# Recurrence in one round per seed pair: seeds for two rounds in one bank, additions split 22 to 10, eight output buffers, and a seam check of two instructions a half

## The chip, the cores and the metric

The kernel runs on one core of one Trainium2 chip. The metric is the time of one execution on the device, in microseconds (us). The engines have short names in the profile: PE is the matrix engine (PEld its weight loads), DVE the vector engine, ACT the scalar engine, POOL the GpSimd engine, SP the engine that issues most of the transfers (DMA). PSUM is the memory that matmuls write to[...]. SBUF is the working memory.

## What is computed

Two layers over `x` of 4 x 128 x 64 x 64. Layer 0 is a windowed attention with a depthwise convolution ahead of it. Layer 1 is a linear attention and then a recurrence over the 4096 tokens of each image, and only this last part is concerned here:

```python
def _L1_ffn_ref(x, W, V, gamma, beta):
    ...
    Wx = jnp.einsum('bti,hi->bth', x, W)
    flat = Wx.reshape(B * T, H)
    mean = jnp.mean(flat, axis=0)
    var = jnp.var(flat, axis=0)
    Wx = ((flat - mean) * jax.lax.rsqrt(var + BN_EPS) * gamma + beta).reshape(B, T, H)
    Vt = V.T
    def step(yt, wx_t):
        yt = jax.nn.sigmoid(wx_t + yt @ Vt)
        return (yt, yt)
    y0 = jnp.zeros((B, H), dtype=Wx.dtype)
    _, ys = jax.lax.scan(step, y0, jnp.swapaxes(Wx, 0, 1))
    return jnp.swapaxes(ys, 0, 1)
...
t = t + _L1_ffn_ref(_ln_t(t), L1_ffn_W, L1_ffn_V, L1_ffn_gamma, L1_ffn_beta)
```

The mean and variance run over all tokens, so the recurrence can't start before the rest of the kernel has ended.

## The kernel before

The first 856 us, up to L733 (`main.close()`), hold layer 0 and the linear attention, in 64 windows whose instructions stand in an order that the kernel fixes for each engine (`in_order`, L732). That part leaves two things behind. `wx` in SBUF holds the products of the recurrence's input, laid out as [channel, image, piece, step, run of 16]. `resd` in device memory holds the values to which the recurrence's outputs are added.

What the diff touches is the rest, from L740 on, whose instructions the build may place by itself within each engine's queue.

**Loads and statistics.** `res` (8 MB) is read back from `resd` by four transfers of one image each (L748), two on SP's queue, two on ACT's. DVE and POOL turn the gathered statistics into a factor `sc` and an offset `shift` for each channel (L754 to L761).

**Cutting the recurrence.** The 4096 steps of an image are cut into 128 segments of 32 steps (`SEGS`, `SEG`). All segments of all four images advance together: one round is one step of 4 x 128 = 512 columns, each with 128 channels on the partitions. Segment k would need the end of segment k-1 as its start, which isn't there yet; so it starts 11 steps (`WARM`) ahead, at step 21 of the segment before, from nothing, and runs 11 warm rounds that produce no output. The state has then forgotten its start. Of the warm result, shifted by one segment (the tiles `warm` have one column more, column 0 being zero for the true start), 32 counted rounds follow. At the end the state reached by each segment is compared with the warm start of the next (the seam): where any differs by more than `TOL`, a flag sends the program to a slower general version (L849), which doesn't run in these executions.

**A round.** The 512 columns are two groups of 256 (`NG`, images 0 and 1, images 2 and 3). For each, DVE writes `wx * sc + shift` of that step into a bank of PSUM (the seed, `seeded`, L771), PE adds the product of the previous state with `fvT` onto it (L803 warm, L815 counted), and ACT writes the sigmoid (L806 and L817), which is the next state. While ACT works on one group, PE can work on the other. A group has three banks, of which a seed uses half. [...]

**Output of a counted round.** POOL adds `res` and `ys` for images 0 to 2 (384 columns), DVE for image 3 (128), into `ot` (L822), and SP sends `ot` to device memory (L823, 256 KB). `ys` and `ot` come from the pool `ring` with three buffers each. An addition waits until the transfer of three rounds before has read its `ot`; a sigmoid waits until the additions of three rounds before have read its `ys`; and DVE takes its instructions in order, so seeds placed behind a waiting addition wait too.

**The end.** For each group DVE runs four instructions of 256 columns: difference, square, comparison, sum (L830 to L833). One small matmul (L840) sums over the partitions, L842 and L844 make the flag `bad`, all engines load it (L847), and the program ends.

## Time and profile before

| what | value |
|---|---|
| median of 6 runs | 931.58 us (927.58 to 934.5) |
| the profiled execution | 930.36 us |
| its span, first to last instruction | 928.5 us |
| PE, DVE, ACT, POOL busy over the span | 94%, 80%, 58%, 28% |
| last transfer of `res` landed | 879.04 us |
| seeds L771 | 86, mean 541 ns (128 x 256) |
| counted sigmoids L817 | 64, mean 385 ns (128 x 256) |
| additions L822, POOL / DVE | 32 each, mean 1080 ns (128 x 384) / 324 ns (128 x 128) |
| seam check L830, L831, L832, L833 | 2 each, mean 522, 750, 286, 413 ns |

The stage of the change by stretches, in us from the span's start. Columns: PE, PEld, DVE, ACT and POOL busy, each with its number of instructions, the TensorE clock that was granted, the DMA engines' busy share, GB/s moved:

```profile
856.50:860.30 3.80, 1.31 (x6) 0.59 (x4) 2.63 (x7) 1.49 (x2) 0.75 (x2) 0.50 0.92 315
860.30:879.90 19.60, 17.34 (x54) 9.25 (x54) 14.89 (x30) 10.80 (x28) 2.89 (x3) 0.87 0.86 368
879.90:888.50 8.60, 7.20 (x26) 3.99 (x26) 8.60 (x22) 4.51 (x12) 5.08 (x5) 1.00 0.49 191
888.50:899.60 11.10, 10.10 (x37) 5.83 (x36) 10.23 (x28) 6.81 (x18) 10.24 (x11) 1.00 0.60 233
899.60:917.50 17.90, 14.61 (x54) 7.82 (x52) 15.32 (x39) 9.97 (x26) 14.30 (x14) 1.00 0.49 192
917.50:922.50 5.00, 0.54 (x4) 0.09 (x2) 4.12 (x11) 0.76 (x2) 1.78 (x2) 0.76 0.40 157
```

The rows are: statistics; warm rounds and the first counted ones, while `res` loads; the rounds just behind that load; the middle; the rest of the rounds; the end. A timeline row gives the start, the time from its first to its last instruction, the engine, the line, what it writes and reads, and in brackets how long the engine was idle before it and what ended that. A row of the chain of waits gives start, length, and the engine and line that the end of the kernel went through.

### The profile page before, as it was taken

To read this page: it belongs to the slowest core of one execution; us is meant where nothing else is said; L and a number is where in the kernel's file an instruction comes from. 1 tells how busy PE (TensorE), PEld (TensorE's weight loads), DVE (VectorE), ACT (ScalarE), POOL (GpSimd) and SP (SyncE) were. 2 spreads that over 40 slices of the span, in tenths; PEclk is the share of its full clock that TensorE was granted. 3 is DMA by queue.
4 is the path that set the end of the run, shared out by engine and by line. 5 is a ranking of instruction groups with operands and counts; after the bars stand their busy time and mean duration, and the time that the engine had idled before them with its cause. 6 is when DMAs were issued, how large, how long until landed. Compare 5 with 4: busy or idle time off the path is not lost.

```text
span 928.5 us, 26534 instructions
## 1 busy us (share of the span) xinstructions
PE 872.0 (94%) x10508; PEld 652.3 (70%) x10508; DVE 740.3 (80%) x2452; ACT 540.1 (58%) x1010; POOL 260.2 (28%) x359
## 2 busy tenths in 40 slices
PE   4978999999999999999999999999999999977884
PEld 3856777777777877777787877787777777755442
DVE  6455979888797978797988889797879786677796
ACT  3655666565756566666656575656666665523553
POOL 2122131423232232313132323223231412121185
PEclk9989999999999999999999999999999999999898
DMA  4112121122212111212112121212121111101853
GB/s 121 28 44 62 37 78 42 48 57 63 60 62 59 50 54 49 73 38 81 41 49 58 59 59 60 60 51 58 48 71 40 58 37 60 32 35 51 349 217 136
DMA packets 53045, 63.46 MB, mean 68 GB/s; under 512 B 22960, under 2 KB 33840, under 8 KB 52400
## 3 DMA queue, kind: packets, MB, share of 16 engines
q1 hardware_dynamic: 51184, 56.91, 19.6%
q10 hardware_dynamic: 1728, 4.77, 1.3%
q8 instruction: 85, 1.39, 0.6%
q14 instruction: 48, 0.39, 0.1%
HBM read 35.44 MB, written 17.30 MB: 57 GB/s over the span
## 4 chain that ended last, share of the span: by engine, by line
PE 60%; DVE 24%; DMA 5%; ACT 4%; issue 3%; POOL 3%; ACTq 0%; DVEq 0%; SPq 0%; POOLq 0%
PE bank L337 8%; DVE y L288 8%; PE bank L382 6%; PE bank L465 6%; PE bank L212 6%; PE bank L494 4%; PE bank L400 4%; PE bank L350 4%; PE bank L412 4%; PE bank L602 3%; DMA res<-resd 2%; PE bank L573 2%; PE bank L537 2%; DVE st L191 2%; PE bank L575 2%
## 5 line engine op out<-in xcount | busy, mean ns | idle before, releaser
L288 DVE SCALAR_TENSOR_TENSOR y<-ypad,cpe_w,y 128x512 f32<-128x512 f32 x240 | 190.5, 794 | 16.8 <-ACT y L286 13.4
L391 ACT ACTIVATE es<-bank 128x512 f32<-128x512 f32 x256 | 132.4, 604 | 76.9 <-PE bank L382 76.9
L440 POOL TENSOR_TENSOR oT<-o_sb,rden 128x512 f32<-128x512 f32 x64 | 84.2, 1316 | 243.2 <-DMA rden<-rd 209.7
L195 POOL TENSOR_SCALAR rs<-mv 128x4 f32<-128x4 f32 (+2 forms) x100 | 25.2, 252 | 364.4 <-DVE mv L193 162.5
L203 DVE TENSOR_SCALAR xn<-x,mv,rs 128x128 f32<-128x128 f32 x256 | 88.8, 409 | 26.6 <-POOL rs L196 26.6
L196 POOL TENSOR_TENSOR rs<-rs,mhalf 128x4 f32<-128x4 f32 (+2 forms) x100 | 106.2, 1062 | 8.3
L382 PEld LDWEIGHTS bank<-q,k 32*128 32x128 f32 x3072 | 97.7, 189 | 9.0 <-ACT k L345 7.8
L382 PE MATMUL bank<-q,k 32*128 32x96 f32 (+1 forms) x3072 | 96.3, 270 | 1.1 <-ACT k L345 1.1
L412 PEld LDWEIGHTS bank<-es,v_sb 128*32 128x32 f32 x3072 | 56.5, 110 | 30.1 <-issue 20.3
L465 PE MATMUL bank<-woT,oT 128*128 128x128 f32 x512 | 65.6, 283 | 6.1 <-POOL oT L440 6.1
L494 PE MATMUL bank<-xl,awT 128*128 128x512 f32 x128 | 70.0, 630 | 0.0
L412 PE MATMUL bank<-es,v_sb 128*32 128x96 f32 (+1 forms) x3072 | 69.7, 239 | 0.0
L465 PEld LDWEIGHTS bank<-woT,oT 128*128 128x128 f32 x512 | 62.4, 196 | 10.2 <-POOL oT L440 7.8
L400 PE MATMUL bank<-es,ones 128*32 128x512 f32 x512 | 69.1, 612 | 0.0
L357 ACT COPY v_sb<-bank 128x512 f32<-128x512 f32 x64 | 37.6, 588 | 53.5 <-PE bank L350 45.7
L337 PE MATMUL bank<-y2w,wqT 128*128 128x256 f32 x256 | 67.3, 386 | 1.0 <-DVE y2w L288 1.0
L337 PE MATMUL bank<-y2w,wkT 128*128 128x256 f32 x256 | 66.7, 384 | 0.0
L350 PE MATMUL bank<-wvT,y2w 128*128 128x256 f32 x256 | 66.0, 380 | 0.0
L345 ACT COPY q<-bank 128x512 f32<-128x512 f32 x64 | 37.7, 589 | 40.8 <-PE bank L337 38.9
L345 ACT COPY k<-bank 128x512 f32<-128x512 f32 x64 | 37.4, 585 | 37.5 <-PE bank L337 37.4
L191 DVE BATCH_NORM_STATS2 st<-x 128x6 f32<-128x128 f32 x256 | 55.5, 280 | 1.1
L337 PEld LDWEIGHTS bank<-y2w,wqT 128*128 128x128 f32 x256 | 46.1, 195 | 13.0 <-issue 7.2
(124 smaller groups left out, 1725.1 us busy)
## 6 DMA issues: line engine op xcount, KB each, us to landing
rden<-rd SPq DMA_DIRECT2D x64, 256.0 KB
v_sb<-v_sb SPq DMA_DIRECT2D x128, 64.0 KB
resd<-rs_o SPq DMA_DIRECT2D x32, 256.0 KB
out<-ot SPq DMA_DIRECT2D x32, 256.0 KB
xin<-in_xt SPq DMA_DIRECT2D x15, 512.0 KB
res<-resd SPq DMA_DIRECT2D x2, 2048.0 KB
res<-resd ACTq DMA_DIRECT2D x2, 2048.0 KB
dc<-den SPq DMA_DIRECT2D x64, 8.0 KB
```

The source lines that it names most:

```text
L196: nc.gpsimd.tensor_tensor(rs[:, :n], rs[:, :n], mhalf[:, :n], ALU.pow)
L203: nc.vector.tensor_scalar(xn[:, j, :], piece, mv[:, j, 0:1], rs[:, j : j + 1], ALU.subtract, ALU.mult)
L288: nc.vector.scalar_tensor_tensor(y2, src, cpe_w[:, tap : tap + 1], y2, ALU.mult, ALU.add)
L337: nc.tensor.matmul(pps[:, br * WT : (br + 1) * WT], wT[:, br * P : (br + 1) * P], y2, start=True, stop=True,)
L350: nc.tensor.matmul(vps[:, e * 256 : (e + 1) * 256], y2[:, e * P : (e + 1) * P], wvT, start=True, stop=True,)
L382: nc.tensor.matmul(sps[h][:, cols], w["k"][rows, k0 : k0 + P], w["q"][rows, cols], start=False, stop=(br, n) == pieces[-1],)
L391: nc.scalar.activation(es, sps[h], AF.Exp, scale=scale)
L400: nc.tensor.matmul(dps[rows], ones[:, :HD], w["es", h], start=True, stop=True)
L412: nc.tensor.matmul(ops[rows, cols], w["v"][:, n, c0 : c0 + HD], w["es", h][:, cols], start=(br, n) == pieces[0], stop=(br, n) == pieces[-1],)
L440: nc.gpsimd.tensor_tensor(oTs[n][:, :, :, wj * WS : (wj + 1) * WS], w["o"].rearrange("p (a r c) -> p a r c", a=BR, c=WS), w["rden"].rearra ...
L465: nc.tensor.matmul(yps[:, j * P : (j + 1) * P], oT[:, br, t], woT[:, br, :], start=br == 0, stop=br == BR - 1,)
L494: nc.tensor.matmul(zps, awT[:, m * P : (m + 1) * P], h.xl, start=True, stop=True)
```

## The change

- The first warm round is a sigmoid of ACT straight from `wx`, with `sc` and `shift` as its factor and offset; it has no seed.
- The other 10 warm and the 32 counted rounds stand in one list, `rounds`. For two rounds that follow each other, a group has one seed: one DVE instruction of 512 columns fills both halves of a bank, and the two rounds use a half each. A group still has three banks, seeded in the order of the pairs, up to two pairs ahead in the program's text. The other pool of PSUM has one bank for two.
- Warm rounds write into `ys` of the ring too; only the last of them writes `warm`, which is one tile now, and the `spare` tiles are gone.
- The additions are split by rows of 16 columns: POOL takes 22 of 32 rows (352 columns), DVE 10 (160).
- `ot` has eight buffers. `ys` still has three.
- The seam is compared by two instructions a group, each `(end + TOL >= warm)` or `(end - TOL <= warm)` with the sum of the ones as a second output (`accum_out`). The count that is expected becomes twice as large.

```diff
--- before.py
+++ after.py
@@ -740,8 +740,9 @@
     sp = fast.enter_context(tc.tile_pool(name="sp", bufs=1))
     rec = ExitStack()
     ring = rec.enter_context(tc.tile_pool(name="ring", bufs=3))
-    ps_r = rec.enter_context(tc.tile_pool(name="ps_r", bufs=3, space=PSUM))
-    ps_m = rec.enter_context(tc.tile_pool(name="ps_m2", bufs=2, space=PSUM))
+    ZBUFS = 3
+    ps_r = rec.enter_context(tc.tile_pool(name="ps_r", bufs=ZBUFS, space=PSUM))
+    ps_m = rec.enter_context(tc.tile_pool(name="ps_m2", bufs=1, space=PSUM))
 
     res = sp.tile([P, B, NH, SEG, HSEGS], F32, name="res")
     for b in range(B):
@@ -760,77 +761,108 @@
     nc.vector.tensor_tensor(shift, mv[:, 0:1], sc, ALU.mult)
     nc.vector.tensor_tensor(shift, beta, shift, ALU.subtract)
 
-    NG = 2
-    GB = B // NG
-    GC = GB * SEGS
-
-    def seeded(g, s):
-
-
-        bk = ps_r.tile([P, 512], F32, tag=f"bank{g}", name=f"bank{g}")
-        nc.vector.tensor_scalar(
-            bk[:, :GC].rearrange("p (b n k) -> p b n k", n=NH, k=HSEGS),
-            wx[:, g * GB : (g + 1) * GB, :, s, :],
-            sc,
-            shift,
-            ALU.mult,
-            ALU.add,
-        )
-        return bk[:, :GC]
+
+    rounds = [(s, False) for s in range(SEG - WARM + 1, SEG)] + [(s, True) for s in range(SEG)]
+    COLS = B * SEGS
+    GC = COLS // 2
+    seeds = {}
+
+    def seed(k, g):
+
+
+        if 2 * k < len(rounds):
+            s = rounds[2 * k][0]
+            seeds[k, g] = ps_r.tile([P, 2, GC], F32, tag=f"z{g}", name=f"z{g}")
+            nc.vector.tensor_scalar(
+                seeds[k, g].rearrange("p r (m k) -> p r m k", k=HSEGS),
+                wx[:, 2 * g : 2 * g + 2, :, s : s + 2, :].rearrange("p b n s k -> p s (b n) k"),
+                sc,
+                shift,
+                ALU.mult,
+                ALU.add,
+            )
 
 
     idle = sp.tile([P, 1], F32, name="idle")
     nc.scalar.activation(idle, ones[:, :1], AF.Sigmoid)
 
 
-    for g in range(NG):
-        for _ in range(3):
-            bk = ps_r.tile([P, 512], F32, tag=f"bank{g}", name=f"bank{g}")
+    for _ in range(ZBUFS):
+        for g in range(2):
+            bk = ps_r.tile([P, COLS], F32, tag=f"z{g}", name=f"z{g}")
             nc.tensor.matmul(
-                bk[:, :GC], zeros, zeros[:, :1].to_broadcast([P, GC]), start=True, stop=True
-            )
-
-
-    warm = [sp.tile([P, GB, SEGS + 1], F32, name=f"warm{g}") for g in range(NG)]
-    spare = [sp.tile([P, GB, SEGS + 1], F32, name=f"spare{g}") for g in range(NG)]
-    for g in range(NG):
-        nc.gpsimd.memset(warm[g][:, :, 0:1], 0.0)
-    for s in range(SEG - WARM, SEG):
-        for g in range(NG):
-            z = seeded(g, s)
-            now, was = (warm[g], spare[g]) if (SEG - 1 - s) % 2 == 0 else (spare[g], warm[g])
-            if s > SEG - WARM:
-                nc.tensor.matmul(
-                    z, fvT, was[:, :, 1:], start=False, stop=True, skip_group_check=True
+                bk, zeros, zeros[:, :1].to_broadcast([P, COLS]), start=True, stop=True
+            )
+
+
+    warm = sp.tile([P, B, SEGS + 1], F32, name="warm")
+    nc.gpsimd.memset(warm[:, :, 0:1], 0.0)
+    halves = [(0, GC), (GC, COLS)]
+
+    last = ring.tile([P, COLS], F32, tag="ys", name="ys")
+    for c0, c1 in halves:
+        nc.scalar.activation(
+            last[:, c0:c1].rearrange("p (m k) -> p m k", k=HSEGS),
+            wx[:, c0 // SEGS : c1 // SEGS, :, SEG - WARM, :].rearrange("p b n k -> p (b n) k"),
+            AF.Sigmoid,
+            bias=shift,
+            scale=sc,
+        )
+    for k in range(ZBUFS - 1):
+        for g in range(2):
+            seed(k, g)
+    for r, (s, counts) in enumerate(rounds):
+        seed(r // 2 + ZBUFS - 1, r % 2)
+
+        moved, were_moved = rounds[r] == (SEG - 1, False), rounds[r] == (0, True)
+        ys = None if moved else ring.tile([P, COLS], F32, tag="ys", name="ys")
+        for g, (c0, c1) in enumerate(halves):
+            b = slice(c0 // SEGS, c1 // SEGS)
+            z = seeds[r // 2, g][:, r % 2, :]
+            nc.tensor.matmul(
+                z,
+                fvT,
+                warm[:, b, :SEGS] if were_moved else last[:, c0:c1],
+                start=False,
+                stop=True,
+                skip_group_check=True,
+            )
+            if moved:
+                nc.scalar.activation(
+                    warm[:, b, 1:], z.rearrange("p (b k) -> p b k", k=SEGS), AF.Sigmoid
                 )
-            nc.scalar.activation(
-                now[:, :, 1:], z.rearrange("p (b k) -> p b k", k=SEGS), AF.Sigmoid
-            )
-
-    last = [w[:, :, :SEGS] for w in warm]
-    for s in range(SEG):
-        ys = ring.tile([P, B * SEGS], F32, tag="ys", name="ys")
-        for g in range(NG):
-            z = seeded(g, s)
-            nc.tensor.matmul(z, fvT, last[g], start=False, stop=True, skip_group_check=True)
-            y = ys[:, g * GC : (g + 1) * GC]
-            nc.scalar.activation(y, z, AF.Sigmoid)
-            last[g] = y
-        ot = ring.tile([P, B, NH, HSEGS], F32, tag="ot", name="ot")
-        yv = ys.rearrange("p (b n k) -> p b n k", n=NH, k=HSEGS)
-        for eng, b0, b1 in ((nc.gpsimd, 0, 3), (nc.vector, 3, 4)):
-            eng.tensor_tensor(ot[:, b0:b1], res[:, b0:b1, :, s, :], yv[:, b0:b1], ALU.add)
-        nc.sync.dma_start(out[s].rearrange("p b k -> p (b k)"), ot.rearrange("p b n k -> p (b n k)"))
-
-
+            else:
+                nc.scalar.activation(ys[:, c0:c1], z, AF.Sigmoid)
+        if not moved:
+            last = ys
+        if counts:
+            ot = ring.tile([P, COLS], F32, tag="ot", name="ot", bufs=8)
+            for eng, m0, m1 in ((nc.gpsimd, 0, 22), (nc.vector, 22, 32)):
+                eng.tensor_tensor(
+                    ot.rearrange("p (m k) -> p m k", k=HSEGS)[:, m0:m1],
+                    res[:, :, :, s, :].rearrange("p b n k -> p (b n) k")[:, m0:m1],
+                    ys.rearrange("p (m k) -> p m k", k=HSEGS)[:, m0:m1],
+                    ALU.add,
+                )
+            nc.sync.dma_start(out[s].rearrange("p b k -> p (b k)"), ot)
+
+
+
+    NG = 4
     okc = sp.tile([P, NG + 1], F32, name="okc")
-    for g in range(NG):
-        d = sp.tile([P, GB, SEGS], F32, tag="d", name="d", bufs=2)
-        end = last[g].rearrange("p (b k) -> p b k", k=SEGS)
-        nc.vector.tensor_tensor(d, end, warm[g][:, :, 1:], ALU.subtract)
-        nc.vector.tensor_tensor(d, d, d, ALU.mult)
-        nc.vector.tensor_scalar(d, d, TOL * TOL, None, ALU.is_le)
-        nc.vector.tensor_reduce(okc[:, g : g + 1], d, AX.XY, ALU.add)
+    d = sp.tile([P, COLS], F32, name="d")
+    for i, (b0, b1) in enumerate(((0, 2), (2, B))):
+        end = last[:, b0 * SEGS : b1 * SEGS].rearrange("p (b k) -> p b k", k=SEGS)
+        for k, (side, op) in enumerate(((ALU.add, ALU.is_ge), (ALU.subtract, ALU.is_le))):
+            nc.vector.scalar_tensor_tensor(
+                d[:, b0 * SEGS : b1 * SEGS].rearrange("p (b k) -> p b k", k=SEGS),
+                end,
+                TOL,
+                warm[:, b0:b1, 1:],
+                side,
+                op,
+                accum_out=okc[:, 2 * i + k : 2 * i + k + 1],
+            )
 
     nc.vector.tensor_scalar(dmax, dmax, HUGE, None, ALU.is_le)
     nc.vector.tensor_scalar(dmin, dmin, TINY, None, ALU.is_ge)
@@ -841,7 +873,7 @@
     oks = sp.tile([1, 1], F32, name="oks")
     nc.vector.tensor_reduce(oks, okp[:1, : NG + 1], AX.X, ALU.add)
     bad = sp.tile([1, 1], mybir.dt.int32, name="bad")
-    nc.vector.tensor_scalar(bad, oks, float(P * B * SEGS + P * 16), None, ALU.is_lt)
+    nc.vector.tensor_scalar(bad, oks, float(2 * P * B * SEGS + P * 16), None, ALU.is_lt)
     rec.close()
 
     flag = nc.values_load(bad[0:1, 0:1], min_val=0, max_val=1)
```

## The prediction

> **What bounds the kernel now.** I read the page's engine table and slices first: PE is 94% busy over the whole span, but the slices after about 856 us fall to 7 and 8, so the last 72 us, which is all that the change touches, have another limit. Then the chain of waits for that stretch:
>
> ```profile
> 856.43 22.61 DMA res<-resd
> ...
> 879.13 0.74 DVE ot L822
> ...
> 900.55 1.11 POOL ot L822
> ...
> 901.68 3.83 DMA out<-ot
> ...
> 905.64 0.29 DVE ot L822
> 905.93 0.47 DVE bank L771
> ```
>
> The reader is to see two gates. Up to 879.04 us the load of `res` is last, whatever the rounds do. Later the chain goes twice through an output transfer (3.83 us here, 2.63 us at 909.33), then through DVE's addition and a seed queued behind it. Next, ACT's timeline, which counts rounds (a round is two sigmoids):
>
> ```profile
> 874.05 0.89 ACT L806 ACTIVATE warm<-bank 128x256 f32<-128x256 f32 x2 [0.29 <-PE bank L803]
> 875.25 0.89 ACT L817 ACTIVATE ys<-bank 128x256 f32<-128x256 f32 x2 [0.30 <-PE bank L815]
> 876.42 0.89 ACT L817 ACTIVATE ys<-bank 128x256 f32<-128x256 f32 x2 [0.29 <-PE bank L815]
> 877.59 0.89 ACT L817 ACTIVATE ys<-bank 128x256 f32<-128x256 f32 x2 [0.29 <-PE bank L815]
> 879.99 0.39 ACT L817 ACTIVATE ys<-bank 128x256 f32<-128x256 f32 x1 [1.51 <-DVE ot L822]
> ...
> 898.37 0.76 ACT L817 ACTIVATE ys<-bank 128x256 f32<-128x256 f32 x2 [0.47 <-PE bank L815]
> 899.65 0.77 ACT L817 ACTIVATE ys<-bank 128x256 f32<-128x256 f32 x2 [0.52 <-PE bank L815]
> ...
> 904.70 0.77 ACT L817 ACTIVATE ys<-bank 128x256 f32<-128x256 f32 x2 [0.52 <-PE bank L815]
> 907.30 0.78 ACT L817 ACTIVATE ys<-bank 128x256 f32<-128x256 f32 x2 [1.83 <-PE bank L815]
> ...
> 917.51 0.76 ACT L817 ACTIVATE ys<-bank 128x256 f32<-128x256 f32 x2 [0.46 <-PE bank L815]
> ```
>
> Warm rounds come every 1.17 us. Three counted rounds (s = 0, 1, 2) are done when ACT stops, for `ys` has three buffers and the first is held by an addition that waits for `res`. From s = 3 at 879.99 to s = 31 at 917.51 there are 28 periods in 37.52 us, 1.340 each. Undisturbed ones, 889.74 to 898.37, are 1.233; later short (1.23) and long (1.29) ones alternate, the idle time before them 0.46 and 0.52. One takes 2.60 (904.70 to 907.30). The first six after 879.99 hold 8.51 us, 1.10 more than six of 1.233: DVE then has seeds and additions to catch up on.
>
> Last, DVE's timeline at the end:
>
> ```profile
> 917.93 0.63 DVE L830 TENSOR_TENSOR d<-ys,warm 128x256 f32<-128x256 f32 x1 [0.50 <-ACT ys L817]
> 918.59 1.09 DVE L831 TENSOR_TENSOR d<-d 128x256 f32<-128x256 f32 x1
> 919.60 0.28 DVE L822 TENSOR_TENSOR ot<-res,ys 128x128 f32<-128x128 f32 x1
> ...
> 921.44 0.42 DVE L833 TENSOR_REDUCE okc<-d 128x1 f32<-128x256 f32 x1
> ...
> 922.33 0.14 DVE L844 TENSOR_SCALAR bad<-oks 1x1 int32<-1x1 f32 x1
> ```
>
> Call T the end of the last sigmoid, 917.51 + 0.76 = 918.27. The flag is written at 922.47, T + 4.2; then come 6.0 us of flag load, branch and closing that the change leaves alone (span 928.5).
>
> [...] L831 took 1.09 us beside POOL's last addition (918.40 to 919.40) and 0.41 without it, while seeds beside POOL keep 0.53 to 0.55. [...] In the 3.83 us wait, fifteen of the sixteen had landed by 903.68 and the last at 905.52: a straggler, which a deeper ring absorbs, not a lack of bandwidth. [...] Here L288, that operation without an accumulator, takes 794 ns for 512 columns; no run yet shows it with one.
>
> **Part by part.** *The start.* The first round loses its seeds: ACT takes the sigmoid from `wx` directly once `shift` is there (859.62) instead of at 860.36. Two seeds of 512 columns follow, then round two. A 512-column seed isn't in the trace. The 256-column one takes 541 ns, 470 start to start (4.70 us for ten). DVE's additions grow from 292 ns at 128 columns to 413 at 256, 0.945 ns a column, so 541 + 242 = 783 ns, some 710 start to start. Bounds: 610 (half of the growth) and 940 start to start (twice the old). The first matmul can start at about 860.5, its sigmoid at 861.25, and ten warm periods later, at 873.0, the first counted one: 2.2 us before 875.25. All of it is lost against the load of `res`, which still lands at 879.04: ACT's stop grows from 1.5 to about 3.7 us. I cost the start at nothing. The zeroing matmuls write 512 columns for 256, at most doubling 1.44 us on PE, to 857.8 plus 1.4: they end before the first seed. One POOL memset less is idle time.
>
> *Restart at `res`.* DVE's waiting addition has 160 columns for 128: 292 + 32 x 0.945 = 322 ns, here 0.74 + 0.03 beside POOL. ACT restarts at 880.0 as before, at s = 3.
>
> *DVE in a round.* Before: two seeds and an addition, 2 x 0.45 + 0.20 = 1.10 us start to start, of a period of 1.233: hardly room to catch up. After: one seed and a longer addition, 0.71 + 0.23 = 0.94. Seeds may run up to six rounds ahead instead of three. Of 86 seeds 42 remain. So the catching up of 1.10 us should go: PE finds its seeds ready for the first rounds behind the stop, and DVE has 0.29 us of slack a round. If that slack weren't there, the 1.10 would come back.
>
> *POOL.* 352 columns for 384: between 990 (in proportion) and 1080 ns. It has three rounds before its `ys` is written again, so this saves nothing on the path.
>
> *Eight output buffers.* An addition waits for the transfer of eight rounds before, not three: five more periods, 6.2 us, against a straggler of 1.9. The 2.60 becomes 1.23 (1.37 less), and the 1.40 at 912.35 also (0.17).
>
> *What is late next.* The loop PE, ACT, PE of group 0: sigmoid 0.39, 0.05, load and matmuls 0.70, 0.04, plus 0.06 for a second wait that ACT's first sigmoid of a counted round takes as an instruction of its own, after PE's last matmul. That second wait (for the additions that read `ys`) stays, so 1.233 and not 1.17. The long 1.29 comes where PE's extra wait instruction stands ahead of the weight load. Only every other round of a group waits for a new seed now, so I take the middle of 1.233 and the alternating mean 1.26: 1.247. 28 x (1.340 - 1.247) = 2.6 us less up to T.
>
> *The end.* Eight comparing instructions become four with an accumulator. One of 256 columns is 794 - 256 x 0.945 = 552 ns, about 0.5 start to start[...]. In the order seen before (one on group 0, the second held by POOL's last addition until T + 1.42, DVE's addition, then group 1) : T + 1.5, + 0.25, + 2 x 0.56, + 0.6 for the count on PE and its two small instructions (921.86 to 922.47) is T + 3.4, so 0.8 less. Bounds: [...] T + 2.6 where POOL doesn't hold DVE: 0.1 to 1.6 less. The last transfer would land near T + 3.8, which the closing 6 us cover.
>
> Sum: 2.6 + 0.8 = 3.4 us. The profiled execution took 930.36 (span 928.5 and 1.9 around it): 927.0. The median shown is 931.58, 1.2 above that execution, so 928.2.
>
> **Rivals.**
> - *The loop gets faster* (1.17 a round): half of PE's seed waits go, and the order of ACT's waits may change. For: warm rounds run so, with the same matmuls. Against: the wait for the additions stays. 28 x 0.17 + 0.8 = 5.5 less: 926.1.
> - *The rounds stay slow* at about 1.30, because PE's and ACT's extra waits, not DVE, make the long ones, and the end gives 0.3: 28 x 0.04 + 0.3 = 1.4 less: 930.2. For: the alternation occurs where DVE isn't late. Against: 1.37 us of one stall are plainly a transfer's.
> - *DVE becomes the bound*: slower. Its place is the seed in two pieces of `wx`, written to PSUM. [...] It decides above a seed of 1.0 us start to start (1.233 - 0.23). For: nobody has timed it here. Against: [...] twice the old one is still only 0.94.
>
> **How the numbers follow.** About 0.3%, 2.8 us, can be told from no change. Chances: forecast 0.61, faster loop 0.12, slow rounds 0.20, DVE bound 0.07. The forecast's own spread from the end (0.1 to 1.6) and the period (1.233 to 1.26) is 2.3 to 4.6 us less, so a third of it falls within 0.3%: faster 0.64, same 0.27, slower 0.09. The range takes in the faster loop and the slow rounds with the median's own scatter, and leaves out most of the DVE case: 924.5 to 931.0.
>
> **What would show it.** L771's successor: 42 of about 0.78 us. ACT's stop ahead of s = 3 near 3.7 us, ending at 880.0. No wait of DVE or POOL on `out<-ot`, periods near 1.25 from there, T near 915.7. Four comparing instructions near 0.55 us, the flag 3.4 after T. Seeds over 1.0 us or a restart later than 880.5 would make it wrong, as would periods at 1.17 or 1.30.

## The result, and the profile after

| | median | runs |
|---|---|---|
| before | 931.70 us | 38 |
| after | 927.08 us (923.69 to 931.52) | 17 |
| ratio after / before | 0.9952, 95% interval 0.994 to 0.9964 | |

The change makes the kernel faster by 0.36 to 0.6%, 4.5 us at the ratio itself. 928.2 had been forecast.

The profiled execution of after took 929.61 us with a span of 927.9, only 0.6 us below the span of before. It can't be compared by its span: the part that the change leaves alone ended 1.8 us later in it (last copy to `wx` at 858.11 us, before 856.32), and its close after the flag took 7.45 us (before 6.06). So from here on I count from the end of the last copy to `wx` ("main"), in three stretches: to the first sigmoid of s = 3, on to the end T of the last sigmoid, on to the flag written. Each is read off the timelines as before. For all kernels of this study (ratios against the runs of before on the same chip):

| kernel | median us | ratio, interval | main to s = 3 | s = 3 to T | T to flag | sum |
|---|---|---|---|---|---|---|
| before | 931.70 | | 23.66 | 38.28 | 4.21 | 66.15 |
| after | 927.08 | 0.9952 (0.994, 0.9964) | 23.32 | 35.99 | 3.00 | 62.32 |
| e1, three output buffers | 930.17 | 0.9987 (0.9967, 1.0008) | 23.52 | 38.35 | 3.65 | 65.52 |
| e2, before with eight output buffers | 940.70 | 1.009 (1.0059, 1.012) | 23.89 | 47.14 | 4.21 | 75.24 |
| x1, e2 with POOL only writing | 927.88 | 0.9957 (0.9939, 0.9975) | 22.98 | 36.23 | 3.26 | 62.47 |
| x2, e2 with 22 to 10 | 931.07 | 0.9991 (0.9971, 1.0011) | 23.93 | 38.65 | 4.15 | 66.73 |
| e7, after with 24 to 8 | 928.61 | 0.9944 (0.9925, 0.9963) | 23.21 | 36.02 | 3.05 | 62.28 |
| e3, a seed for each round | 928.94 | 0.997 (0.9951, 0.9988) | 23.56 | 37.44 | 3.00 | 64.00 |
| e6, PE kept at work in the stop | 926.35 | 0.994 (0.9923, 0.9958) | 23.61 | 34.97 | 3.00 | 61.57 |
| e9, e3 and e6 | 932.29 | 0.9986 (0.9971, 1.0002) | 23.63 | 39.11 | 3.00 | 65.73 |
| e10, e9 with PE's work moved | 927.86 | 0.996 (0.9948, 0.9972) | 23.18 | 36.52 | 3.00 | 62.70 |
| e4, the old seam comparison | 929.19 | 0.996 (0.9947, 0.9974) | 23.36 | 36.00 | 4.16 | 63.52 |
| e5, eight `ys` buffers | 925.73 | 0.9941 (0.992, 0.9962) | 21.48 | 35.32 | 3.00 | 59.80 |
| e8, e5 with PE kept at work at the start | 925.38 | 0.991 (0.9888, 0.9932) | 20.35 | 36.51 | 3.00 | 59.85 |

After against before in the profiled executions: 0.34 + 2.29 + 1.21 = 3.8 us less. The other 0.7 us of the 4.5 is not traced to anything: each column comes from one execution of each kernel.

The chain of waits of after, with start, length, engine and line. L835 is the counted sigmoid, L822 the matmul, L841 the addition, L776 the seed:

```profile
858.22 22.44 DMA res<-resd
...
880.78 0.55 DVE ot L841
...
881.43 0.39 ACT ys L835
...
881.87 4.20 PE z L822 x10
...
896.80 1.07 POOL ot L841
```

The first gate is unchanged: the load of `res`, 22.4 us (before 22.6). Behind it the chain no longer goes through any transfer of `out<-ot`. But there is a piece that was not in the chain of before: PE works for 4.20 us without a pause right behind the stop. ACT's timeline shows what that does to the rounds:

```profile
881.43 0.66 ACT L835 ACTIVATE ys<-z 128x256 f32<-128x256 f32 x2 [2.22 <-DVE ot L841]
882.65 0.38 ACT L835 ACTIVATE ys<-z 128x256 f32<-128x256 f32 x1 [0.56 <-PE z L822]
883.33 0.38 ACT L835 ACTIVATE ys<-z 128x256 f32<-128x256 f32 x1 [0.30 <-PE z L822]
884.39 0.38 ACT L835 ACTIVATE ys<-z 128x256 f32<-128x256 f32 x1 [0.68 <-PE z L822]
...
886.13 0.79 ACT L835 ACTIVATE ys<-z 128x256 f32<-128x256 f32 x2 [0.55 <-PE z L822]
887.35 0.77 ACT L835 ACTIVATE ys<-z 128x256 f32<-128x256 f32 x2 [0.43 <-PE z L822]
...
916.66 0.77 ACT L835 ACTIVATE ys<-z 128x256 f32<-128x256 f32 x2 [0.45 <-DVE ot L841]
```

Periods from s = 3 on are 1.22, 1.74, 1.74 and then 1.22 to the end: 25 times, with neither the 1.29 nor the 2.60 of before. From 895.90 on ACT's release is put down to DVE's addition, as in the last row, and from there the chain runs over the additions (its last row above). That can't be so: the sigmoid at 916.66, of s = 31, waits only for the additions of three rounds before, s = 28, and these had ended at 914.18 (DVE) and 914.96 (POOL). The addition that is named is that of s = 30, which happens to end at 916.62. So PE's matmul releases ACT there too, after the same 0.45 us, and the additions are off the path. The period is 1.22 with either name in the row, and 1.23 in e5 below, where a sigmoid needs only the additions of eight rounds before. The table by stretches, with the granted clock ahead of the DMA share, says why two are 1.74:

```profile
882.56:885.97 3.41, 3.41 (x10) 2.00 (x9) 3.41 (x7) 1.53 (x4) 1.77 (x3) 0.50 0.57 214
885.97:900.00 14.03, 12.97 (x48) 7.19 (x46) 13.45 (x24) 8.86 (x24) 11.07 (x12) 1.00 0.59 223
```

For 3.41 us PE had half the clock (0.50). Two rounds fall into it and take 0.52 longer each, 1.04 us that the forecast sum doesn't have.

The end, DVE's timeline (L857 is the seam comparison):

```profile
917.07 0.61 DVE L857 SCALAR_TENSOR_TENSOR d<-ys,warm 128x256 f32<-128x256 f32 x1 [0.46 <-ACT ys L835]
917.61 0.08 DVE L857 DVE_READ_ACCUMULATOR d<-ys,warm 128x1 f32 x1
917.73 1.03 DVE L857 SCALAR_TENSOR_TENSOR d<-ys,warm 128x256 f32<-128x256 f32 x1
...
918.69 0.32 DVE L841 TENSOR_TENSOR ot<-res,ys 128x160 f32<-128x160 f32 x1
918.92 0.42 DVE L857 SCALAR_TENSOR_TENSOR d<-ys,warm 128x256 f32<-128x256 f32 x1
...
919.38 0.43 DVE L857 SCALAR_TENSOR_TENSOR d<-ys,warm 128x256 f32<-128x256 f32 x1
...
920.29 0.14 DVE L876 TENSOR_SCALAR bad<-oks 1x1 int32<-1x1 f32 x1
```

The order is the forecast one: one comparison, the second held by POOL's last addition (1.03 for 0.42), DVE's addition, the other two. The flag is written at 920.43, T + 3.0.

### The profile page after: what moved, and what is told of

The parts are those of the page before. It is cut to its first block, busy times and chain, and to the rows that moved or that the text cites. A ratio compares the mean times of both kernels' runs of the same rounds, so it can differ in the third digit from the quotient of the medians.

```text
span 927.9 us, 26460 instructions
## 1 busy us (share of the span) xinstructions
PE 876.2 (94%) x10508; PEld 655.0 (71%) x10508; DVE 733.5 (79%) x2408; ACT 539.5 (58%) x1010; POOL 258.0 (28%) x358
## 4 chain that ended last, share of the span: by engine, by line
PE 56%; DVE 27%; ACT 5%; DMA 4%; issue 4%; POOL 3%; ACTq 0%; DVEq 0%; POOLq 0%; SPq 0%
DVE y L288 9%; PE bank L337 8%; PE bank L465 6%; PE bank L382 6%; PE bank L212 6%; PE bank L494 4%; PE bank L400 4%; PE bank L350 4%; PE bank L412 4%; PE bank L602 3%; DMA res<-resd 2%; DVE st L191 2%; DVE f L499 2%; PE bank L573 2%; PE bank L537 2%
## 5 line engine op out<-in xcount | busy, mean ns | idle before, releaser
L288 DVE SCALAR_TENSOR_TENSOR y<-ypad,cpe_w,y 128x512 f32<-128x512 f32 x240 | 190.8, 795 | 16.9 <-ACT y L286 13.4
```

Source lines behind the costliest of these rows:

```text
L288: nc.vector.scalar_tensor_tensor(y2, src, cpe_w[:, tap : tap + 1], y2, ALU.mult, ALU.add)
```

## The experiments

### Output buffers

**e1**: the changed kernel with three output buffers.

```diff
-            ot = ring.tile([P, COLS], F32, tag="ot", name="ot", bufs=8)
+            ot = ring.tile([P, COLS], F32, tag="ot", name="ot", bufs=3)
```

> The changed kernel with three output buffers in place of eight. My theory: additions wait again for straggling transfers, once or twice, 1.0 to 2.0 us in all, so some 928.6 us (0.997 of the kernel before); in the profile DVE and POOL wait for out<-ot after the 20th counted round and a period of 2 us or more stands among those of 1.22. Rival (the eight buffers are worth nothing, seeds and the end hold the whole gain): no such wait, 927.1.

Measured 930.17 us: by the ratios 0.35%, 3.3 us, slower than after. The waits of POOL and DVE (total us, times, longest):

```profile
POOL ot L841 <- DMA out<-ot: 4.0, 3, 2.5
```

```profile
DVE ot L841 <- DMA out<-ot: 1.6, 3, 1.0
```

Six of its 28 periods are late (1.49, 2.10, 1.87, 1.69, 1.70, 1.95, against 1.22 for the others), 3.5 us together. There is no half clock behind its stop, so its 38.35 compares with the 34.97 of e6: 3.4 us. So in the changed kernel eight buffers are worth 3.3 to 3.4 us, twice what the prediction gave them (1.37 + 0.17). Late transfers alone don't explain it: from issue to landing they take 2.21 us on average in e1 and 2.20 in before, and two of 32 take over 3 us in each. In e1 the additions fall behind at the restart: POOL's of s = 3 has its buffer only 1.5 us after its sigmoid (0.1 in after), and four of DVE's seven additions from there to s = 9 run beside POOL's and take 0.85 to 1.04 us. Five of the six late sigmoids start within 0.13 us of the end of the DVE addition that they wait for. The sixth, the last, waits for one of POOL's, and that one for a transfer of 3.59 us. How much the waits for buffers and how much the contention of the two engines costs is not separated.

**e2**: before, with eight output buffers and nothing else.

```diff
-        ot = ring.tile([P, B, NH, HSEGS], F32, tag="ot", name="ot")
+        ot = ring.tile([P, B, NH, HSEGS], F32, tag="ot", name="ot", bufs=8)
```

> The kernel before with eight output buffers alone. My theory: its waits for out<-ot (1.37 and 0.17 us) go, 1.5 us less than before: 930.2. The long rounds of 1.29 and the catching up behind the load of res stay. Rival (a late transfer is only what shows, DVE is what is short): the time stays 931.7, with DVE late in its place.

A plain miss: 940.70 us, 0.9% slower than before. From s = 10 to s = 27 the rounds take 1.71 us. POOL's timeline, and then DVE's, of two such rounds:

```profile
901.49 0.99 POOL L822 TENSOR_TENSOR ot<-res,ys 128x384 f32<-128x384 f32 x1 [0.71 <-ACT ys L817]
903.20 1.00 POOL L822 TENSOR_TENSOR ot<-res,ys 128x384 f32<-128x384 f32 x1 [0.72 <-ACT ys L817]
```

```profile
900.85 0.98 DVE L771 TENSOR_SCALAR bank<-wx,sc,shift 128x256 f32<-128x256 f32 x2
901.74 0.88 DVE L822 TENSOR_TENSOR ot<-res,ys 128x128 f32<-128x128 f32 x1
902.55 0.98 DVE L771 TENSOR_SCALAR bank<-wx,sc,shift 128x256 f32<-128x256 f32 x2
903.44 0.90 DVE L822 TENSOR_TENSOR ot<-res,ys 128x128 f32<-128x128 f32 x1
```

POOL starts its addition at 901.49, DVE its own 0.25 later, and DVE's takes 0.88 us where it takes 0.29 alone: it ends 0.14 after POOL's (902.48). The next seeds stand behind it in DVE's queue and start at 902.55, and PE waits for them (0.58 us idle, ended by the seed). That puts the next round's additions in the same order, and so on: a loop that keeps itself up. DVE has no idle time in it: its two seeds and the held addition are the 1.71. The loop also ends within this trace. At s = 27 POOL's addition starts some 0.3 us later than in the rounds before, for no reason that the trace shows, and so just behind DVE's:

```profile
922.27 1.08 POOL L822 TENSOR_TENSOR ot<-res,ys 128x384 f32<-128x384 f32 x1 [1.01 <-ACT ys L817]
```

```profile
922.23 0.27 DVE L822 TENSOR_TENSOR ot<-res,ys 128x128 f32<-128x128 f32 x1
```

From s = 28 on the periods are 1.23 to 1.29, with the same buffers and the same split. These rows suggest two things: that POOL's reading holds DVE, and that the order of the starts decides who is held. The traces of x1 and x2 agree with both (0.28 to 0.29 us for DVE's addition beside POOL's writes; 0.33 for DVE and 1.06 for POOL where DVE starts first).

**x1**: e2, but POOL writes zeros to its part of `ot` instead of adding. The outputs of images 0 to 2 are left out.

```diff
-        for eng, b0, b1 in ((nc.gpsimd, 0, 3), (nc.vector, 3, 4)):
-            eng.tensor_tensor(ot[:, b0:b1], res[:, b0:b1, :, s, :], yv[:, b0:b1], ALU.add)
+        nc.gpsimd.memset(ot[:, 0:3], 0.0)
+        nc.vector.tensor_tensor(ot[:, 3:4], res[:, 3:4, :, s, :], yv[:, 3:4], ALU.add)
```

> The kernel before with eight output buffers, and in place of POOL's addition a memset of its three images in ot (those outputs are left out; POOL reads nothing of SBUF). My theory of the 1.71 us rounds of the eight-buffer kernel (POOL's addition holds DVE's, 0.89 instead of 0.29 us, and the seeds of the round after next stand behind it): DVE's addition takes 0.29, periods 1.23 to 1.30, about 929 us. Rival (DVE's order alone, one round of seeds ahead, makes them): 1.6 us and more remain, 937 or more.

927.88 us, and the series of 1.71 is gone: periods of 1.17 to 1.30, with two of 1.66 and 1.53 near the restart. So POOL's addition makes the slow rounds of e2, not the buffers, the transfers or PE. The memsets don't wait for `ys` and so come at other times than the additions did; but 19 of DVE's 32 additions ran beside one of them, and all 32 took 0.28 to 0.29 us. It is POOL's reading, then, and not its being at work, that holds DVE.

**x2**: e2 with the additions split 22 to 10.

```diff
-        for eng, b0, b1 in ((nc.gpsimd, 0, 3), (nc.vector, 3, 4)):
-            eng.tensor_tensor(ot[:, b0:b1], res[:, b0:b1, :, s, :], yv[:, b0:b1], ALU.add)
+        for eng, m0, m1 in ((nc.gpsimd, 0, 22), (nc.vector, 22, 32)):
+            eng.tensor_tensor(
+                ot.rearrange("p b n k -> p (b n) k")[:, m0:m1],
+                res[:, :, :, s, :].rearrange("p b n k -> p (b n) k")[:, m0:m1],
+                ys.rearrange("p (m k) -> p m k", k=HSEGS)[:, m0:m1],
+                ALU.add,
+            )
```

> The kernel before with eight output buffers and the additions split 22 to 10. My theory (what decides is how many rounds of seeds stand ahead of an addition in DVE's queue: 1 here, as in the eight-buffer kernel, 2 in the one with a seed for each round, 5 in the changed one): rounds of about 1.65 us, since POOL's shorter addition holds DVE 0.07 us less, 937 to 940. Rival (the split keeps DVE out of POOL's way): 1.23 to 1.30, about 930.

Another miss: 931.07 us. Some rounds behind the restart are long (up to 2.39), but from s = 8 on they take 1.23 and 1.32 in turn, and no series of 1.71 begins. POOL's and DVE's timelines:

```profile
907.32 1.06 POOL L822 TENSOR_TENSOR ot<-res,ys 128x352 f32<-128x352 f32 x1 [0.27 <-ACT ys L817]
```

```profile
907.27 0.33 DVE L822 TENSOR_TENSOR ot<-res,ys 128x160 f32<-128x160 f32 x1
907.51 0.99 DVE L771 TENSOR_SCALAR bank<-wx,sc,shift 128x256 f32<-128x256 f32 x2
```

Here DVE starts 0.05 us ahead of POOL. It then takes 0.33, and POOL bears it with 1.06 for the 0.92 that its 352 columns take alone. So which of the two starts first decides between rounds of 1.23 to 1.32 and of 1.71, as it does within e2 at s = 27, and the same buffers can be worth nothing or cost 8 us. The expectation, that a lead of one round is enough to lock, was wrong: x2 has that lead, and doesn't lock.

**e7**: the changed kernel with the old split.

```diff
-            for eng, m0, m1 in ((nc.gpsimd, 0, 22), (nc.vector, 22, 32)):
+            for eng, m0, m1 in ((nc.gpsimd, 0, 24), (nc.vector, 24, 32)):
```

> The changed kernel with the additions split 24 to 8 as before (POOL 384 columns, DVE 128) instead of 22 to 10. Theory (how far DVE's seeds stand ahead of its additions decides whether rounds lock at 1.71 us; with one seed for two rounds they stand five rounds ahead, so the split doesn't matter): periods behind the stop stay at 1.22 to 1.23, median within 1.5 us of the changed kernel's 927.1, POOL's addition about 1.08 us. Rival (the split is what keeps DVE from being held by POOL, as eight buffers with 24 to 8 took 940.7 us and with 22 to 10 took 931.1): rounds of 1.71 us return, 933 to 936 us.

As the theory had it: the ratio is that of after within its interval, and s = 3 to T 36.02 against 35.99. DVE's timeline:

```profile
900.40 0.59 DVE L841 TENSOR_TENSOR ot<-res,ys 128x128 f32<-128x128 f32 x1
900.91 0.80 DVE L776 TENSOR_SCALAR z<-wx,sc,shift 128x512 f32<-128x512 f32 x1
```

DVE's addition is still held in each round (0.58 for 0.29), and it costs nothing: in DVE's order the seeds stand five rounds ahead of the additions in this kernel (in e2 one round, from s = 8 on), and a round of DVE's just fits (0.51 from 900.40 to 900.91, and 0.71 to the next addition at 901.62). So the new split did nothing for the changed kernel. What keeps it from locking is not separated: the longer lead of its seeds, or DVE's smaller work on them (0.71 us a round for some 0.9 in e2, so that a held addition still fits). e3 below has the new split, a seed for each round and a lead of two rounds, and doesn't lock either (DVE's addition 0.41, rounds of 1.23).

### Seeds and the clock behind the stop

**e6**: the changed kernel with two fp32 matmuls whose result nobody reads.

```diff
+        if rounds[r] == (2, True):
+            held = ys
+        if rounds[r] == (3, True):
+            junk = ps_m.tile([P, COLS], F32, tag="junk", name="junk")
+            for _ in range(2):
+                nc.tensor.matmul(junk, fvT, held, start=True, stop=True)
```

> The changed kernel with two matmuls of 512 columns (float32) on the state of s = 2, whose result nobody reads, ahead of those of s = 3: they fill PE's idle time while ACT waits for res. My theory: no window of half clock follows, the two periods of 1.74 become 1.22 (1.04 us less), and s = 3 starts up to 0.3 us later: 926.3. Rival (the slow periods are DVE's, catching up): they stay, and the time is 927.1 to 927.4.

One correction: in the built order the two stand behind the matmuls of s = 3 and ahead of those of s = 4, which are the ones that wait at the stop. PE's timeline:

```profile
873.11 3.68 PE L822 MATMUL z<-ys,fvT 128*128 128x256 f32 x12
876.62 1.88 PE L841 MATMUL junk<-ys,fvT 128*128 128x512 f32 x4
878.79 3.57 PE L822 MATMUL z<-ys,fvT 128*128 128x256 f32 x12 [0.29 <-ACT ys L835]
```

PE's pause shrinks to 0.29 us, the clock stays at 1.00 from s = 3 on (34.97 us), and all periods are 1.22: 1.02 us less than after for more work. What the half clock costs is shown by that. That the added matmuls kept it away is not, for e1 has the pause of after, no added matmuls, and full clock as well:

```profile
878.75 4.58 PE L822 MATMUL z<-ys,fvT 128*128 128x256 f32 x15 [1.90 <-ACT ys L835]
```

What differs is where the pause falls: the clock changed on a grid of 3.41 us in these traces (last section; a window is one piece of the grid), and in after a window that began 2.3 us ahead of s = 3 was 56% idle, in e1 one that began 0.9 us ahead was 42% idle. e6's began 0.9 us ahead too, and without the added matmuls it would have been 42% idle as well, an estimate from its other matmuls. That PE's idle time is the cause is better shown by e9 and e10 below. By the ratios e6 gains 0.1%, 1.1 us, on after, with overlapping intervals; how often the half clock occurs wasn't counted. Among the profiled executions with a pause of this length after, e4 and e7 have it, e1 doesn't.

**e3**: a seed of 256 columns for each round and group.

```diff
-        if 2 * k < len(rounds):
-            s = rounds[2 * k][0]
-            seeds[k, g] = ps_r.tile([P, 2, GC], F32, tag=f"z{g}", name=f"z{g}")
+        if k < len(rounds):
+            s = rounds[k][0]
+            seeds[k, g] = ps_r.tile([P, COLS], F32, tag=f"z{g}", name=f"z{g}")
...
-        seed(r // 2 + ZBUFS - 1, r % 2)
+        for g in range(2):
+            seed(r + ZBUFS - 1, g)
```

> The changed kernel with a seed of 256 columns for each round and group, in half of a bank, as before: 84 seeds instead of 42, three rounds ahead instead of six. My theory: DVE has 1.13 us of work in a period of 1.22, so the catching up behind the load of res (1.1 us) and some rounds of 1.29 come back: 1.3 us more than the changed kernel, 928.4. Rival (PE's slow clock, not DVE, makes the slow rounds behind the stop): those two rounds are slow or not as the clock has it, and the time is 927.1 plus at most 0.5.

928.94 us, by the ratios 1.7 us slower than after, though the intervals overlap; from s = 3 to T it is 1.45. Periods from s = 3: 2.62, 1.75, 1.49, then 1.23. DVE's timeline and PE's:

```profile
880.04 0.52 DVE L842 TENSOR_TENSOR ot<-res,ys 128x160 f32<-128x160 f32 x1 [5.46 <-DMA res<-resd]
880.49 0.98 DVE L776 TENSOR_SCALAR z<-wx,sc,shift 128x256 f32<-128x256 f32 x2
```

```profile
875.77 1.34 PE L823 MATMUL z<-ys,fvT 128*128 128x256 f32 x4
881.17 4.22 PE L823 MATMUL z<-ys,fvT 128*128 128x256 f32 x9 [4.06 <-ACT ys L836]
```

With three seeds a group, one a round, a seed of s = 3 stands behind the addition that waits for `res`. PE stops for 4.06 us instead of 1.9, the half clock lasts two windows, 6.83 us (879.21 to 886.04), and then come the seeds. Two causes at once, so e9 and e10 take the clock away.

**e9**: e3 with the two matmuls of e6.

```diff
+        if rounds[r] == (2, True):
+            held = ys
+        if rounds[r] == (3, True):
+            junk = ps_m.tile([P, COLS], F32, tag="junk", name="junk")
+            for _ in range(2):
+                nc.tensor.matmul(junk, fvT, held, start=True, stop=True)
```

> The changed kernel with a seed of 256 columns for each round and group, as before the change, and with two additional fp32 matmuls of 512 columns on the state of s = 2 into a bank that nothing reads, which keep PE at work during the stop before s = 3. It takes the half clock behind the stop out of the comparison of seeds. Theory (with a seed a round DVE has seeds to catch up on behind the stop, 1.10 us in all): no half-clock window behind the stop, the first six periods behind it hold about 1.1 us more than six of 1.23, and the time is about 1 us above the 926.35 of the same matmuls with seeds for two rounds. Rival (DVE catches up within the stop; what cost time there was the half clock alone): all periods behind the stop at 1.22 to 1.25 and no difference.

Neither: 932.29 us. In PE's queue the matmuls stood behind the one that waits for the seed, so they ran after the stop (884.75 to 888.33) at half clock, 3.58 us where e6's took 1.88, and held up the rounds: the period of s = 3 is 5.09. The run says nothing of the theory.

**e10**: the same with four of them, between the two groups' matmuls of s = 3.

```diff
+        if rounds[r] == (3, True):
+            junk = ps_m.tile([P, COLS], F32, tag="junk", name="junk")
+            for _ in range(4):
+                nc.tensor.matmul(junk, fvT, last, start=True, stop=True)
         for g, (c0, c1) in enumerate(halves):
```

> Seeds of 256 columns for each round and group in the changed kernel, as in e9, but the additional matmuls (four fp32 ones of 512 columns on the state of s = 2) now stand in PE's queue between the two groups' matmuls of s = 3, where PE waits for a seed that stands behind DVE's held addition; in e9 they stood behind that wait and ran after the restart. So PE works through most of the stop. Theory (DVE has seeds to catch up on behind the stop, and that costs about 1.1 us, the half clock the rest of what e3 loses): no half-clock window from the stop on, from the first sigmoid of s = 3 to the last one 36 to 36.5 us (37.44 in e3, 34.97 with seeds for two rounds and PE kept busy), first six periods about 1.1 us more than six of 1.23. Rival (only the clock made the periods behind the stop long): 35.0 to 35.3 us, all periods 1.22 to 1.25.

The clock stays at 1.00 from s = 3 to T, and this shows that the half clock behind this stop comes from PE's idle time: the added matmuls fill the window from 877.42 to 880.83 (3.41 us of work), while in e9, where they came too late, the last window of the stop (881.34 to 884.75) held 0.50 us of work and half clock followed. From s = 3 to T it takes 36.52 us, as the theory said; but the trace doesn't let the theory count as shown. PE's timeline:

```profile
877.40 3.70 PE L823 MATMUL junk<-ys,fvT 128*128 128x512 f32 x8
880.94 4.48 PE L827 MATMUL z<-ys,fvT 128*128 128x256 f32 x15
```

The seed that PE needed was written at 879.88, but the added matmuls ran until 880.94, 1.06 later; in e3 PE started 0.15 behind the same seed. So about 0.9 us of the 1.55 that e10 has over e6 are theirs. All but 0.25 of the 1.55 lies in one period of 2.52, ahead of 1.22s; the 0.25 are 1.23 for 1.22 in the later ones. That leaves DVE's catching up some 0.4 us at full clock in the changed kernel, an estimate, and not 1.1. Theory and rival both stay unproved, and the run shows that the half clock, which it took away, is the larger part of what e3 loses: 36.52 less the 0.9 is 35.6, against 37.44.

### The end

**e4**: the old seam comparison (difference, square, comparison, sum for each group).

```diff
-            nc.vector.scalar_tensor_tensor(
...
-                accum_out=okc[:, 2 * i + k : 2 * i + k + 1],
-            )
+        nc.vector.tensor_tensor(d, end, warm[:, 2 * g : 2 * g + 2, 1:], ALU.subtract)
+        nc.vector.tensor_tensor(d, d, d, ALU.mult)
+        nc.vector.tensor_scalar(d, d, TOL * TOL, None, ALU.is_le)
+        nc.vector.tensor_reduce(okc[:, g : g + 1], d, AX.XY, ALU.add)
```

> The changed kernel with the four comparing instructions a half of before. My theory: the flag is written 4.2 us after the last sigmoid instead of 3.0, so 1.2 us more than the changed kernel, 928.3. Rival (the closing or the last transfer hides the end): 927.1.

T to flag is 4.16 for 3.00, 1.16 us, and all other stretches are those of after within 0.05 (it has the half clock, too). The ratios differ by 0.08%, 0.7 us, which their intervals don't tell from nothing; the trace shows it.

### What is left: the stop and the start

**e5**: the changed kernel with eight `ys` buffers.

```diff
-    last = ring.tile([P, COLS], F32, tag="ys", name="ys")
+    last = ring.tile([P, COLS], F32, tag="ys", name="ys", bufs=8)
...
-        ys = None if moved else ring.tile([P, COLS], F32, tag="ys", name="ys")
+        ys = None if moved else ring.tile([P, COLS], F32, tag="ys", name="ys", bufs=8)
```

> The changed kernel with eight buffers for ys instead of three, so that sigmoids need not wait for the additions that wait for res. My theory: the stop of 2.2 us ahead of s = 3 goes, and with it PE's idle time and the window of half clock behind it (1.04 us in the changed kernel's trace): 3 us less from the end of the main part to the flag, 924.1 us. Rival (the additions, which can't start before res, are late at the end instead): the last sigmoid is earlier but POOL's and DVE's additions end where they ended, and the time stays 927.1.

925.73 us. The rounds run on while `res` loads, there is no stop and no half clock behind it: 2.5 us less than after from main to flag. ACT's timeline, s = 7 to s = 9:

```profile
882.87 0.39 ACT L835 ACTIVATE ys<-z 128x256 f32<-128x256 f32 x1 [0.19 <-PE z L822]
...
884.10 0.39 ACT L835 ACTIVATE ys<-z 128x256 f32<-128x256 f32 x1 [0.25 <-PE z L822]
...
885.34 0.86 ACT L835 ACTIVATE ys<-z 128x256 f32<-128x256 f32 x2 [0.31 <-PE z L822]
```

The period goes from 1.17 to 1.23 exactly at s = 8, the first round that uses a buffer again and so waits for additions. It isn't the additions that are late there: those of s = 0, which s = 8 waits for, had ended at 879.74. ACT takes that wait as an instruction of its own, 0.06 us on the loop, in this kernel from s = 8 and in after from s = 3. This run also shows that eight output buffers absorb a late transfer: that of s = 24 took 3.96 us to land, and no addition waited for it. The longest of after took 2.96.

**e8**: e5 with four matmuls of zeros ahead of those at L793.

```diff
+    junk = ps_m.tile([P, COLS], F32, tag="junk", name="junk")
+    for _ in range(4):
+        nc.tensor.matmul(
+            junk, zeros, zeros[:, :1].to_broadcast([P, COLS]), start=True, stop=True
+        )
```

> The changed kernel with eight ys buffers, and four additional bf16 matmuls of zeros (512 columns each, into a bank that nothing reads) ahead of the zeroing matmuls, so that PE has work between the end of the main part and the first round. Theory (the first rounds take 2.2 and 1.7 us because TensorE's clock falls to half while PE has little to do between the main part and the recurrence): the half-clock window behind the end of the main part goes, the first rounds take about 1.2 us, and the time is 1 to 1.5 us below the 925.7 of eight ys buffers alone, 924.2 to 924.7. Rival (the window is set by other work, the short loads of the statistics for instance, or the added matmuls delay the first round by as much as the clock gives): 925.7 or above.

The first step came as said: s = 0 comes 16.83 us after main instead of 17.96, and the clock is full for good from 3.5 us after main on instead of 9.3. That the added matmuls did it isn't shown, for in e3, without any, it was full from 1.6 us after main on, up to the stop. But s = 3 to T is 36.51 instead of 35.32, so nothing is left of it in the trace. DVE's timeline, then PE's (lines moved by five, L846 being the addition):

```profile
881.23 0.53 DVE L846 TENSOR_TENSOR ot<-res,ys 128x160 f32<-128x160 f32 x1 [5.14 <-ACT ys L840]
881.68 0.80 DVE L776 TENSOR_SCALAR z<-wx,sc,shift 128x512 f32<-128x512 f32 x1
```

```profile
882.63 0.67 PE L827 MATMUL z<-ys,fvT 128*128 128x256 f32 x2 [0.78 <-DVE z L776]
883.60 2.80 PE L827 MATMUL z<-ys,fvT 128*128 128x256 f32 x9 [0.29 <-DVE z L776]
```

The rounds ran out of seeds: the next ones stood in DVE's queue behind an addition that waited for `res`, the same order that stops e3. (The row names ACT, whose sigmoids of s = 0 had ended at 876.41; the last transfer of `res` landed at 881.11.) The load is the gate again, from the other side. e8 and e5 have the lowest times of the study; both have ratios below that of after, e8 with an interval that lies wholly below after's. That e8 beats e5 isn't shown.

## Why the prediction was right

The direction, the size and the main mechanism held, but its two terms hit for partly wrong reasons.

- **The start, cost at nothing.** Right in effect: s = 3 came 23.32 us after main, before 23.66. The first sigmoid came 0.72 earlier, as worked out (0.74). But s = 0 came 1.1 us earlier and not 2.2: the first two periods were 2.22 and 1.71, for PE had half the clock there, in before as well (0.50 from 855.25 to 865.49 us in both traces); I had taken 1.17 for all of them. In e3, where the clock was full sooner, s = 0 came 2.4 earlier than in before. The two sigmoids straight from `wx` took 0.59 each, where the first ones of before took 0.39. So ACT's stop was 2.22, not 3.7. All of it was lost against `res`, as said.
- **Seeds.** Right: 42 of 808 ns on average, 720 start to start (783 and 710 forecast, from the growth of the additions). The rival with DVE as the bound, which needs 1.0, falls.
- **Catching up, 1.10 us.** Gone, as forecast, from the first six periods of e6 (7.33 us, before 8.51). In after they hold 8.37: the half clock took 1.04 back. What I had read as too many seeds was partly something else: at 883.66 before's DVE addition took 0.73 us, held by POOL's, with the seeds behind it. And with a seed for each round the changed kernel would lose about 0.4 to it (the estimate from e10), so the shared seed isn't all of the gain.
- **Eight buffers, 1.54 us.** Right that the 2.60 goes and that no wait on `out<-ot` is left, though no transfer in the profiled execution of after was as late as the 3.83 us of before. The size holds only for a subtraction from before. Put back alone it costs 3.3 us (e1); put in alone it costs 8 us (e2). The gain of the parts isn't a sum, and the prediction treated it as one.
- **The period.** 1.247 forecast as a mean between 1.233 and 1.26; measured 1.22 throughout, and 35.23 us for 28 with the half clock, 1.258. 2.3 us less where 2.6 was forecast: the error in the steady period (28 x 0.026 = 0.7) and the clock's 1.04 nearly cancelled, which is luck. That the wait stays and so 1.17 doesn't come was right, and e5 shows the mechanism. The alternation to 1.29 is gone; e3, e9 and e10 don't show it either (1.23 steady, seeds two rounds ahead of the additions), before, x1 and x2 do (one round ahead, in before from s = 16 on). So the lead, not half as many seed waits, goes with it; no run changes the lead alone.
- **POOL's 352 columns, nothing on the path.** Right; e7 shows that the whole split is worth nothing here.
- **The end, 0.8 us.** 1.21 in the profiled execution (1.16 by e4), inside the bounds of 0.1 to 1.6, of which the lower was the author's estimate, from an assumed rate that no trace showed. The terms of the forecast add up to T + 3.5 rather than 3.4, and T + 3.0 came. Two terms were too large by 0.2 us each: the held comparison let DVE go at T + 1.27, not 1.5, and the two free comparisons, forecast at 0.56 each start to start, took 0.46: 0.42, and 0.08 for the read of the accumulator, which the trace shows as an instruction of its own. The trace of before had the operation, scalar_tensor_tensor, at this width (L288 at 256 columns, 16 times, 485 ns on average); the 552 was worked out from 512 columns instead. The sum as a second output doesn't make the comparison longer than a plain subtraction: 0.42 us for 256 columns, where the subtraction of the same columns takes 0.41 in e4.
- **Closing, 6.0 us that the change leaves alone.** It varied from 6.06 to 7.93 between the kernels of this study, without any tie to an edit. It belongs to the scatter, and no term of a sum made from one execution can hold better than that.

What the prediction had no term for is the half clock behind the stop, 1.04 us of the profiled execution. Neither rival on the loop came: rounds of 1.17 are kept out by the wait's own instruction, rounds of 1.30 didn't occur where the seeds had two rounds of lead or more. The chances were not added up right: a third of the forecast's 0.61 and all of the slow rounds' 0.20 (1.4 us less) lie within 0.3% of before, which makes 0.40 for no change, not 0.27.

## What to carry to other kernels

A buffer count, a split and an order of seeds are not separate terms where two engines contend for reads: ask for each which instruction starts first, and what stands behind the one that is held. Where an engine's in-order queue has the feed of the critical loop behind an instruction that may wait, write down two numbers: the lead of the feed in rounds, and the engine's work in a round when that instruction is held. With five rounds of lead and 1.22 us of work (e7) a held addition was harmless; with one round and 1.71 (e2) it cost 0.48 us in each round. Where PE must pause, ask what clock it comes back with (0.50 for 3.41 us in after). And where a row names a releaser, look whether the instruction waits for that one at all.

## What the runs showed of the hardware

- **The clock changed on a grid of 3.41 us.** In after the granted clock was 0.50 from 855.25 to 865.49 us, three times 3.41, and from 882.56 to 885.97, once; in before from 855.25 to 865.49; in e3 from 879.21 to 886.04, twice. In before and in after all changes of the clock lie on one grid through the execution. Behind the stop, windows of this grid that were 56 to 62% idle (after, and two of e3; worked out from the matmuls' records) were followed by half clock, windows that were 40 and 42% idle (before, e1) were not. At other places it goes otherwise: in before a window of 43% (from 851.84) was followed by half clock and others of 49 and 46% (from 848.43 and 903.04) were not; in after windows of 24 and 35% (from 855.25 and 858.67), at half clock themselves, were. So no threshold is claimed. Of two pauses of 1.9 us, that of after cost 1.04 us and that of e1 nothing; that the place in the grid decides this is the author's reading, which no run tests by itself.
- **Two SBUF readers, two outcomes.** DVE's 128 columns take 0.27 us when they start first (e2, at 922.23) and 0.88 when POOL starts 0.25 us ahead (e2, at 901.74); POOL's 352 columns, when they start just behind DVE's 160, lose only 0.14 (0.92 to 1.06, x2). A POOL instruction that only writes held none of the 19 additions that it ran beside (x1). Which of them came first went with a whole loop locked at 1.71 us (e2) or rounds of 1.23 to 1.32 (x2).
- **One program, a main part that moves.** The end of the part that all these kernels share lay between 854.75 and 861.25 us in the profiled executions. Differences of a few microseconds are read from one point of the trace to another, not from spans.
